# A four-layer graph network on one Trainium2 core: two partial products of layer 0 made between the column sums, and a quarter's tail rows loaded early into two other places

## The chip, the core and the metric

The kernel runs on one core of a Trainium2 chip. A core has a matrix engine (TensorE, PE in the profile), a vector engine (VectorE, DVE), a scalar engine (ScalarE, ACT), a general engine (GpSimd, POOL), and SyncE (SP), which here does nothing but issue transfers. Each has its own instruction queue and works through it in order; DMA engines move data beside them. The metric is the time of one launch in microseconds (us); smaller is better.

## The reference

x is 2708 x 512 and adj is 2708 x 2708, both float32. Four layers follow one another, each adding to x:

```
h = relu(layernorm(x)); x = x + L0(h)    # four times, L0 to L3
L0: deg = adj.sum(1); dinv = (deg+1)^-0.5
    relu( (dinv * (adj + I) * dinv) @ h @ W0 )
L1: (deg^-.5 * adj * deg^-.5) @ h @ W1.T + b1
L2: relu( ((adj+I) scaled by rsqrt of its row sums) @ h @ W2 )
L3: gated sum of attention(adj, h) @ (h W_sa) and adj @ (h W_gcn) + b
```

The large work is (adj + I) @ h, 2708 x 2708 by 2708 x 512, in each layer. In layer 0 the sums of adj's rows are needed before the first product, since h is scaled by them.

## The kernel before

The nodes are cut into four quarters of 677 (five tiles of 128, and a tail of 37 rows that two extra tail tiles collect). The transposed adjacency lies in memory in blocks of 128 x 5 x 339: a quarter of the rows by half a quarter of the columns; the half is called u, 0 or 1. Each layer's product is done by a scheme with seven products of half matrices in place of eight (the outer products 1 to 7: quarters' sums by quarters' sums), and in each of these, for each u, by the same scheme again: `multiply` makes seven inner products. It opens with product 1 in the bank `pa`, then 6 in `pb`, 2 added to `pa`, 7 in `pc`, 5 in `pd`, 4 added to `pc`, 3 added to `pd`. One inner product is five matmuls, recorded as ten, all at L498. `inner_x` (L445) makes the sums s1 to s4 of pieces of h on VectorE, `inner_y` (L461) the sums t1 to t4 of four adjacency blocks. The names XA to XD are views of h; outer product 1 works with XA, whose first half is made of quarter 0's h (five tiles) and whose second half is quarter 1's.

Layer 0 is written out by hand (`first_aggregate`, L637). For quarters 0 and 1 and each u, `degrees` (L315) sums the columns of the adjacency blocks as they are loaded, by matmuls with `first` (L292) into the bank `dg_ps`. `first_h` (L356) turns these sums into columns by one-column matmuls `pd` (L363), makes the scales on VectorE and then h on ScalarE (L223). Blocks for later sums are formed by transfers: `accumulated` (L670) loads a block with a SyncE transfer (L422) and then adds a second block to it with an accumulating GpSimd transfer (L678); VectorE adds the identity where it is wanted (L430), and GpSimd stores the result for later layers (`keep_o`, L418). Places for blocks come from a list `free`.

The tail rows of the adjacency are added to outer products in `tails` (L579): `tail_rows` loads a quarter's rows, both u at once, by two SyncE transfers of 678 columns (L568) into a block from `free`, VectorE adds the identity (L576), TensorE makes four products for each u in four banks `pt` (L554, L559), and VectorE adds these to `agg` (L597). In layer 0 that happens for quarters 0 and 1 between outer products 4 and 5, into the two y22 places; after it, the four blocks for product 5 and u=1 take `t4[3]`, `more[2]` and the same two places (the line with `t1 = [t2u, ...`).

A scheduler builds the instruction order of each engine from the program text and its priorities. `with tc.issue_after(ins)` adds one rule: what stands inside comes after `ins` if both are on the same engine. Transfers in SyncE's and GpSimd's queues are not bound by it when `ins` is on another engine.

Of the kernel before, what the change touches and what calls it, by code (L numbers as in the profile page):

```python
# [37 lines left out]
def gnn_kernel(  # L38
# [317 lines left out]
    def first_h(columns, looped):  # L356

        ts = list(columns)
        n, t0 = len(ts), ts[0]
        span = slice(t0, t0 + n)  # L360
        pd = ps_sm.tile([P, NT], FP, tag="sm", name="pd")
        for s, t in enumerate(ts):
            nc.tensor.matmul(  # L363
                pd[:, s : s + 1], columns[t], ones[:, 0:1], start=True, stop=True
            )
        if looped:
            nc.vector.tensor_copy(deg[:, t0 : t0 + looped], pd[:, :looped])
        if looped < n:
            nc.vector.tensor_scalar(
                deg[:, t0 + looped : t0 + n], pd[:, looped:n], 1.0, None, ALU.add  # L370
            )
        rsqrt(dinv[:, span], deg[:, span], n)
        mv = mv0[:, span, :]
        rstd = rstd_of(mv, n)
        nc.vector.tensor_mul(rstd[:, :n], rstd[:, :n], dinv[:, span])
        sh = shift_of(mv, rstd, n, at_shift)

        fs = slice(0, D // 2), slice(D // 2, D)
        for f in fs if t0 < half else fs[::-1]:
            for s, t in enumerate(ts):  # L380
                normalized(t, h[:, t, :], rstd[:, s : s + 1], sh[:, s : s + 1], f)
# [59 lines left out]


    at_v, at_u2, at_u3, at_end, at_shift, at_y, at_pe = [], [], [], [], [], [], []

    def inner_x(X):  # L445
# [3 lines left out]
        s1, s2, s3, s4 = (  # L449
            spool.tile([P, U * W], FP, tag=f"s{k}", name=f"s{k}")[:, 0 : KT * P].rearrange(  # L450
                "p (k f) -> p k f", k=KT
            )
            for k in (1, 2, 3, 4)
        )
        nc.vector.tensor_sub(s3, x11, x21)
        minus_sum(s2, x22, s3)
        nc.vector.tensor_sub(s1, x21, x22)
        nc.vector.tensor_add(s4, x12, s2)
        return {1: x11, 2: x12, 3: s4, 4: x22, 5: s1, 6: s2, 7: s3}

    def inner_y(blks, u, loops, t3=None):  # L461
        o11, o12, o21, o22 = blks
        if loops:
            add_loops(o11, u, loops)
            add_loops(o22, u, loops)
        t1, t2, t4 = (tpool.tile([P, KT, W], FP, tag="t", name=f"t{k}") for k in (1, 2, 4))
        t3 = o12 if t3 is None else t3
        nc.vector.tensor_add(t1, o12, o11)
        nc.vector.tensor_add(t2, o22, t1)  # L469
        nc.vector.tensor_add(t4, o21, t2)  # L470
        at_y.append(nc.vector.tensor_add(t3, o22, o12).ins)
        return {1: o11, 2: o21, 3: o22, 4: t4, 5: t1, 6: t2, 7: t3}

    def outer_product(p, self_loops, *dests, at=None):
# [12 lines left out]
            multiply(xs_, ys, u, dests)  # L487
            free.extend(blks)

    def multiply(xs_, ys, u, dests, beside=None):  # L490


        cu = slice(u * W, (u + 1) * W)

        def product(ps, q, start):

            for k in range(KT):
                last = nc.tensor.matmul(  # L498
                    ps, xs_[q][:, k, :], ys[q][:, k, :],
                    start=start and k == 0, stop=k == KT - 1, skip_group_check=not start,  # L500
                )
            at_pe.append(last.ins)

        def bank(name):
            return ps_agg.tile([P, W], FP, tag="agg", name=name)

        def give(a, b, ps, part, op):

            if part is not None and (len(dests) > 1 or dests[0][2] != "as it is"):
                s = upool.tile([P, W], FP, tag="s", name="s")  # L510
                nc.vector.tensor_tensor(s, ps, part, op)
                ps, part = s, None
            for fh, ih, how in dests:
                d = agg[:, fh, ih, a, b, cu]
                if part is not None:
                    at_end.append(nc.vector.tensor_tensor(d, ps, part, op).ins)  # L516
                elif how == "added":
                    at_end.append(nc.vector.tensor_add(d, d, ps).ins)
                elif how == "less":
                    at_end.append(nc.vector.tensor_sub(d, ps, d).ins)  # L520
                else:
                    nc.scalar.copy(d, ps)

        pa = bank("pa")
        product(pa, 1, True)
        v = upool.tile([P, W], FP, tag="v", name="v")
        at_v.append(nc.scalar.copy(v, pa).ins)  # L527
        if beside is not None and beside[0] == 1:
            beside[1]()
        pb = bank("pb")  # L530
        product(pb, 6, True)
        u2 = upool.tile([P, W], FP, tag="u2", name="u2", bufs=2)
        at_u2.append(nc.vector.tensor_add(u2, v, pb).ins)
        product(pa, 2, False)
# [6 lines left out]
        product(pd, 5, True)  # L541
        give(1, 1, pd, u3, ALU.subtract)
        if beside is not None and beside[0] == 5:
            beside[1]()
        product(pc, 4, False)
        give(1, 0, pc, u2, ALU.add)
        product(pd, 3, False)
        give(0, 1, pd, u2, ALU.subtract)

    def tail_products(ps, tl, start):  # L550
# [9 lines left out]
                ps[c], h[g, NF + 1, c * P : (c + 1) * P], tl[g, 1, :], start=False, stop=True  # L560
            )

    def tail_rows(self_loops, q):

        blk = free.pop(0)
        both = blk[:, 0 : 2 * U].rearrange("p (s u) w -> p s u w", s=2)
        for s in range(2):
            nc.sync.dma_start(both[:, s], yt[s, :, q])  # L568
        if self_loops:
            o = (KT * P) % W  # L570
            for s, i, c0, n in (
                (0, ident[:, q * R0 : (q + 1) * R0], o, R0),
                (1, again_ident[:, q * R1P + PAD : (q + 1) * R1P], o + R0, R1),
            ):
                d = both[:, s, U - 1, c0 : c0 + n]
                nc.vector.tensor_add(d, d, i)  # L576
        return blk, both

    def tails(self_loops, qs, loaded=None):  # L579


        at = at_pe[-1]
        for n, q in enumerate(qs):
            blk, both = loaded[n] if loaded else tail_rows(self_loops, q)
            for u in range(U):
                tl = both[:, :, u]
                ps = [
                    (ps_agg if c < NC - 1 else ps_out).tile(
                        [P, W], FP, tag="agg" if c < NC - 1 else "out", name="pt"
                    )  # L590
                    for c in range(NC)
                ]
                with tc.issue_after(at) if loaded else nullcontext():
                    tail_products(ps, tl, True)
                for c in range(NC):
                    d = agg[:, c // 2, q // 2, c % 2, q % 2, u * W : (u + 1) * W]
                    at_end.append(nc.vector.tensor_add(d, d, ps[c]).ins)  # L597
            free.append(blk)

    H1 = list(range(0, half))  # L600
    H2 = list(range(half, NT))
# [35 lines left out]
    def first_aggregate(epilogue):  # L637
# [111 lines left out]
        for u in reversed(range(U)):  # L749
# [47 lines left out]
            if u == 1:  # L797
                free += t4
                with tc.issue_after(at_u3[-1]):
                    nc.vector.tensor_sub(XB, XB, XD)  # L800
        for k, y in ((0, y22[0]), (1, y22[1]), (2, y22[0]), (3, y22[1])):
# [422 lines left out]
```

## Time and profile before

| | |
|---|---|
| time, median of three runs | 2138.92 us (2133.96 to 2140.49) |
| the profiled execution | 2133.39 us |
| its span | 2131.5 us |
| mean granted TensorE clock | 0.994 |
| TensorE matmul busy | 2064.2 us, 97%, 7320 instructions |
| VectorE busy | 1413.2 us, 66% |
| ScalarE busy | 406.0 us, 19% |
| GpSimd busy | 182.4 us, 9% |
| DMA moved | 360.86 MB, 169 GB/s on average |

The profile is one execution, taken by the hardware's profiler. A line of the timeline has the start in us from the span's beginning, the duration in us, the engine (SPq is SyncE's queue of transfers), the line of the kernel, the operation, output<-inputs by name, and the number of like instructions put together; the brackets give the idle time before it and what ended it. A line of the list of waits has the engine, what it wanted to do, who released it, and then total us, number and longest.

### The profile page before, as it was taken

The numbers are of one execution on the slowest core, as the hardware profiler recorded it, in microseconds if no ns is written. First come the engines' busy times: TensorE is split into PE (matmuls) and PEld (weight loads), VectorE is DVE, ScalarE is ACT, GpSimd is POOL, SyncE is SP. The second block draws the span as 40 slices with busy tenths as digits, with TensorE's granted clock in tenths as the row PEclk, the third lists the DMA queues.
The fourth block names the chain that finished last, engine by engine and source line by source line (L and its number), as shares of the span: only waits on it lengthen the run. The fifth ranks groups of instructions, "written<-read, shape, count | busy, mean of one in ns | idle before, by whom it ended". The sixth has DMA issues, their size and how long they took to land.

```text
span 2131.5 us, 20035 instructions
## 1 busy us (share of the span) xinstructions
PE 2064.2 (97%) x7320; PEld 1285.7 (60%) x7320; DVE 1413.2 (66%) x2486; ACT 406.0 (19%) x826; POOL 182.4 (9%) x329
## 2 busy tenths in 40 slices
PE   5999989999999999999999999999999999999997
PEld 2566645546666655666664546666777666666664
DVE  3578857667676767766685879967537755666512
ACT  1340000231000010100002120000117533444401
POOL 1111110120000021100002120000001000000001
PEclk9999999999999999999999999999999999999999
DMA  9998594545555443655454565545551233232212
GB/s 369 298 363 250 187 303 167 189 140 209 175 162 169 151 163 140 235 169 160 164 169 141 203 204 196 182 156 167 176 174 59 95 102 116 79 112 90 83 39 65
DMA packets 79154, 360.86 MB, mean 169 GB/s; under 512 B 10588, under 2 KB 14556, under 8 KB 78928
## 3 DMA queue, kind: packets, MB, share of 16 engines
q1 hardware_dynamic: 50096, 245.43, 33.7%
q0 software_dynamic: 28960, 114.15, 16.5%
q8 instruction: 58, 0.95, 0.2%
q14 instruction: 40, 0.33, 0.0%
HBM read 294.61 MB, written 62.15 MB: 167 GB/s over the span
## 4 chain that ended last, share of the span: by engine, by line
issue 45%; PE 39%; DMA 6%; DVE 5%; POOL 3%; ACT 0%; POOLq 0%; SPq 0%; ACTq 0%; DVEq 0%
PE pa L498 9%; PE pc L498 9%; PE pd L498 9%; PE pb L498 5%; PE po L840 4%; DMA obuf<-in_yb_dram 3%; PE pt L554 2%; DMA ends<-xs 1%; PE pg L979 1%; POOL ends L847 1%; POOL xs L866 1%; DVE ends L932 1%; DMA obuf<-in_yt_dram 1%; POOL out_dram L1083 1%; DMA xs<-ends 1%
## 5 line engine op out<-in xcount | busy, mean ns | idle before, releaser
L1131 PE MATMUL pe<-obuf,h 128*128 128x339 f32 x1280 | 372.8, 448 | 0.0
L498 PE MATMUL pa<-obuf,h 128*128 128x339 f32 x1040 | 318.4, 450 | 5.6 <-ACT h L223 4.2
L1131 PEld LDWEIGHTS pe<-obuf,h 128*128 128x128 f32 x1280 | 240.9, 189 | 126.6 <-issue 10.0
L840 PE MATMUL po<-ends,agg 128*128 128x512 f32 x640 | 281.7, 596 | 5.1 <-ACT ends L860 4.8
L498 PEld LDWEIGHTS pa<-obuf,h 128*128 128x128 f32 x1040 | 196.8, 190 | 111.4 <-issue 8.3
L840 PEld LDWEIGHTS po<-ends,agg 128*128 128x128 f32 x640 | 119.6, 190 | 148.3 <-issue 137.5
L498 PE MATMUL pb<-t,s 128*128 128x339 f32 x560 | 172.8, 455 | 3.4 <-DVE t L469 3.4
L1052 ACT ACTIVATE e<-r,nsr 128x339 f32<-128x339 f32 x352 | 170.7, 566 | 27.7 <-DVE obuf L1056 11.6
L498 PE MATMUL pc<-t,h 128*128 128x339 f32 x560 | 169.4, 448 | 2.8 <-DVE u L539 2.8
L498 PE MATMUL pd<-t,s 128*128 128x339 f32 x560 | 169.2, 447 | 0.0
L498 PE MATMUL pd<-obuf,s 128*128 128x339 f32 x550 | 166.5, 448 | 2.6 <-DVE agg L516 2.6
L527 ACT COPY v<-pa 128x339 f32<-128x339 f32 x56 | 24.6, 440 | 751.0 <-PE pa L498 751.0
L498 PEld LDWEIGHTS pb<-t,s 128*128 128x128 f32 x560 | 107.2, 192 | 59.7 <-DVE t L469 4.4
L498 PEld LDWEIGHTS pc<-t,h 128*128 128x128 f32 x560 | 105.8, 189 | 57.8 <-DVE u L539 3.9
L498 PEld LDWEIGHTS pd<-t,s 128*128 128x128 f32 x560 | 105.9, 189 | 54.4 <-issue 0.5
L498 PEld LDWEIGHTS pd<-obuf,s 128*128 128x128 f32 x550 | 104.0, 189 | 56.6 <-DVE agg L516 4.3
L498 PE MATMUL pc<-obuf,s 128*128 128x339 f32 x440 | 133.1, 448 | 0.0
L498 PEld LDWEIGHTS pc<-obuf,s 128*128 128x128 f32 x440 | 83.3, 189 | 42.8 <-issue 0.5
L469 DVE TENSOR_TENSOR t<-obuf,t 128x1695 f32<-128x1695 f32 x55 | 105.4, 1917 | 0.0
L866 POOL DMA_DIRECT2D xs<-ends x66 | 35.9, 544 | 797.4 <-DVE ends L865 714.9
L470 DVE TENSOR_TENSOR t<-obuf,t 128x1695 f32<-128x1695 f32 x52 | 99.6, 1916 | 0.5 <-PE pc L498 0.5
L1148 DVE COPY agg<-pe 128x339 f32<-128x339 f32 x16 | 7.5, 507 | 138.1 <-PE pe L559 138.1
(251 smaller groups left out, 2291.1 us busy)
## 6 DMA issues: line engine op xcount, KB each, us to landing
obuf<-in_yb_dram SPq DMA_DIRECT2D x132, 847.5 KB, 4.5
obuf<-osumt SPq DMA_DIRECT2D x100, 847.5 KB, 4.5
osumt<-obuf POOLq DMA_DIRECT2D x22, 847.5 KB, 10.2
xs<-ends POOLq DMA_DIRECT2D x66, 256.0 KB, 2.3
ends<-xs POOLq DMA_DIRECT2D x66, 256.0 KB, 3.5
obuf<-in_yt_dram SPq DMA_DIRECT2D x32, 339.0 KB, 3.6
obuf<-in_yb_dram POOLq DMA_DIRECT2D x11, 847.5 KB, 10.8
ends<-in_yb_dram SPq DMA_DIRECT2D x9, 847.5 KB, 9.2
```

The lines of the kernel that those rows point to most:

```text
L469: nc.vector.tensor_add(t2, o22, t1)
L470: nc.vector.tensor_add(t4, o21, t2)
L498: last = nc.tensor.matmul(ps, xs_[q][:, k, :], ys[q][:, k, :], start=start and k == 0, stop=k == KT - 1, skip_group_check=not start,)
L527: at_v.append(nc.scalar.copy(v, pa).ins)
L554: nc.tensor.matmul(ps[c], h[:, NF, c * P : (c + 1) * P], tl[:, 0, :], start=start, stop=False)
L840: nc.tensor.matmul(po, cs[c], w_sb[:, c, :], start=(c == 0), stop=(c == NC - 1))
L847: nc.gpsimd.dma_start(xt, src[t])
L866: nc.gpsimd.dma_start(xs[t], xt)
L932: nc.vector.tensor_tensor_reduce(y, h[:, t, :], vs[:, k, :], 1.0, 0.0, ALU.mult, ALU.add, hd[:, t, k : k + 1])
L979: nc.tensor.matmul(pk, cs[c], wg_sb[:, c, k, :], start=(c == 0), stop=(c == NC - 1))
L1052: nc.scalar.activation(e[:, k], row, AF.Exp, bias=nsr[:, t, s : s + 1], scale=1.0)
L1131: nc.tensor.matmul(pe[c], h[:, t, c * P : (c + 1) * P], a, start=(t == 0), stop=False)
```

## The change

Three things in `first_aggregate`, with the functions they use:

1. After quarter 0's h is made, product 1 of outer product 1 is issued for both u, into two `pa` banks, and s3 is formed at once by the new `inner_x3`. `inner_y` for u=0 makes t3 ahead of t1, and product 7 of u=0 is issued behind the one-column matmuls of quarter 1 (`at_pd`). `multiply` takes these banks as `begun`. For u=1 product 7 is issued ahead of product 6, in a bank of `ps_out`. The degree sums take their banks from `ps_out` instead of `ps_agg`.
2. Quarter 0's tail rows for the first tails are loaded long before, by four transfers of 339 columns (L277): those of u=0 into `left`, those of u=1 into the tile `tl` of the pool `ytp`. Quarter 1's rows take the first of the two y22 places.
3. The last two blocks for product 5, u=1, take the two y22 places in the other order.

```diff
@@ first_h
-            nc.tensor.matmul(
+            last = nc.tensor.matmul(
                 pd[:, s : s + 1], columns[t], ones[:, 0:1], start=True, stop=True
             )
+        at_pd.append(last.ins)
...
+    def inner_x3(X):
+        n = half // 2
+        s3 = spool.tile([P, U * W], FP, tag="s3", name="s3")[:, 0 : KT * P]
+        s3 = s3.rearrange("p (k f) -> p k f", k=KT)
+        nc.vector.tensor_sub(s3, X[:, 0:n, 0:P], X[:, 0:n, P : 2 * P])
+        return s3
...
-    def inner_y(blks, u, loops, t3=None):
+    def inner_y(blks, u, loops, t3=None, t3_first=False):
...
+        if t3_first:
+            nc.vector.tensor_add(t3, o22, o12)
         nc.vector.tensor_add(t1, o12, o11)
         nc.vector.tensor_add(t2, o22, t1)
-        nc.vector.tensor_add(t4, o21, t2)
-        at_y.append(nc.vector.tensor_add(t3, o22, o12).ins)
+        at_y.append(nc.vector.tensor_add(t4, o21, t2).ins)
+        if not t3_first:
+            at_y[-1] = nc.vector.tensor_add(t3, o22, o12).ins
...
-    def multiply(xs_, ys, u, dests, beside=None):
+    def multiply(xs_, ys, u, dests, beside=None, begun=None):
...
-        pa = bank("pa")
-        product(pa, 1, True)
+        pa, pc = begun or (None, None)
+        if pa is None:
+            pa = bank("pa")
+            product(pa, xs_[1], ys[1], True)
...
-        pc = bank("pc")
-        product(pc, 7, True)
+        if pc is None:
+            pc = bank("pc")
+            product(pc, xs_[7], ys[7], True)
...
-    def tail_rows(self_loops, q):
-
-        blk = free.pop(0)
-        both = blk[:, 0 : 2 * U].rearrange("p (s u) w -> p s u w", s=2)
-        for s in range(2):
-            nc.sync.dma_start(both[:, s], yt[s, :, q])
+    def tail_rows(self_loops, q, pieces=None):
+        blk = None
+        if pieces is None:
+            blk = free.pop(0)
+            both = blk[:, 0 : 2 * U].rearrange("p (s u) w -> p s u w", s=2)
+            pieces = [both[:, :, u] for u in range(U)]
+            for s in range(2):
+                nc.sync.dma_start(both[:, s], yt[s, :, q])
+        else:
+            for u in range(U):
+                load_tails(q, u, pieces[u])
...
@@ first_aggregate
-            ps = ps_agg.tile([P, W], FP, tag="agg", name="dg_ps")
+            ps = ps_out.tile([P, W], FP, tag="out", name="dg_ps")
...
+            if (q, u) == (0, 1):
+                pas = [bank("pa") for _ in range(U)]
+                for v in range(U):
+                    product(pas[v], XA[:, 0:KT, 0:P], y11[0, 0, v], True)
+                s3 = inner_x3(XA)
             if (q, u) == (1, 0):
-                ys = inner_y([y11[a, b, u] for a, b in QUAD], u, 0, own_t3)
+                ys = inner_y([y11[a, b, u] for a, b in QUAD], u, 0, own_t3, True)
+        pc = bank("pc")
+        with tc.issue_after(at_pd[-1]):
+            product(pc, s3, ys[7], True)
...
-        xs_ = inner_x(XA)
-        multiply(xs_, ys, 0, [p1])
-        ys = inner_y(blks[1], 1, 0, own_t3)
+        xs_ = inner_x(XA, s3)
+        multiply(xs_, ys, 0, [p1], begun=(pas[0], pc))
+        with tc.issue_after(at_u2[-1]):
+            ys = inner_y(blks[1], 1, 0, own_t3)
...
-        multiply(xs_, ys, 1, [p1])
+        pc = ps_out.tile([P, W], FP, tag="out", name="pc")
+        with tc.issue_after(at_pe[-1]):
+            product(pc, xs_[7], ys[7], True)
+        multiply(xs_, ys, 1, [p1], begun=(pas[1], pc))
...
+                y = ytp.tile([P, 2, W], FP, tag="yt", name="tl")
+                with tc.issue_after(at_end[-1]):
+                    early_rows = tail_rows(
+                        True, 0, [left[:, 0 : 2 * W].rearrange("p (s w) -> p s w", s=2), y]
+                    )
...
-            rows = [tail_rows(True, q) for q in (0, 1)]
+            rows = [early_rows, tail_rows(True, 1)]
         tails(True, (0, 1), rows)
-        t1 = [t2u, [t4[3], more[2]] + [free.pop() for _ in range(2)][::-1]]
+        t1 = [t2u, [t4[3], more[2], free.pop(0), free.pop(0)]]
```

More of the change, by code (lines that the diff above doesn't have):

```diff
@@ L443, in gnn_kernel, with inner_x @@
     at_v, at_u2, at_u3, at_end, at_shift, at_y, at_pe = [], [], [], [], [], [], []
-    def inner_x(X):
+    at_pd = []
+    def inner_x3(X):
[4 more added lines that the diff above has]
+        return s3
+    def inner_x(X, s3=None):
         n = half // 2
@@ L448, in inner_x @@
         x21, x22 = X[:, 0:n, P : 2 * P], X[:, n : 2 * n, P : 2 * P]
-        s1, s2, s3, s4 = (
+        s1, s2, s4 = (
             spool.tile([P, U * W], FP, tag=f"s{k}", name=f"s{k}")[:, 0 : KT * P].rearrange(
@@ L452, in inner_x @@
             )
-            for k in (1, 2, 3, 4)
+            for k in (1, 2, 4)
         )
-        nc.vector.tensor_sub(s3, x11, x21)
+        if s3 is None:
+            s3 = inner_x3(X)
         minus_sum(s2, x22, s3)
@@ L488, in outer_product, with bank, product @@
             free.extend(blks)
-    def multiply(xs_, ys, u, dests, beside=None):
-        cu = slice(u * W, (u + 1) * W)
[L495 to L505, printed above, removed]
+    def bank(name):
+        return ps_agg.tile([P, W], FP, tag="agg", name=name)
+    def product(ps, x, y, start):
+        for k in range(KT):
+            last = nc.tensor.matmul(
+                ps, x[:, k, :], y[:, k, :],
+                start=start and k == 0, stop=k == KT - 1, skip_group_check=not start,
+            )
+        at_pe.append(last.ins)
+    def multiply(xs_, ys, u, dests, beside=None, begun=None):
+        cu = slice(u * W, (u + 1) * W)
         def give(a, b, ps, part, op):
@@ L530, in multiply @@
         pb = bank("pb")
-        product(pb, 6, True)
+        product(pb, xs_[6], ys[6], True)
         u2 = upool.tile([P, W], FP, tag="u2", name="u2", bufs=2)
         at_u2.append(nc.vector.tensor_add(u2, v, pb).ins)
-        product(pa, 2, False)
+        product(pa, xs_[2], ys[2], False)
         give(0, 0, pa, None, None)
-        pc = bank("pc")
-        product(pc, 7, True)
+        if pc is None:
+            pc = bank("pc")
+            product(pc, xs_[7], ys[7], True)
         u3 = upool.tile([P, W], FP, tag="u3", name="u3")
@@ L540, in multiply @@
         pd = bank("pd")
-        product(pd, 5, True)
+        product(pd, xs_[5], ys[5], True)
         give(1, 1, pd, u3, ALU.subtract)
@@ L544, in multiply @@
             beside[1]()
-        product(pc, 4, False)
+        product(pc, xs_[4], ys[4], False)
         give(1, 0, pc, u2, ALU.add)
-        product(pd, 3, False)
+        product(pd, xs_[3], ys[3], False)
         give(0, 1, pd, u2, ALU.subtract)
@@ L574, in tail_rows @@
             ):
-                d = both[:, s, U - 1, c0 : c0 + n]
+                d = pieces[U - 1][:, s, c0 : c0 + n]
                 nc.vector.tensor_add(d, d, i)
-        return blk, both
+        return blk, pieces
     def tails(self_loops, qs, loaded=None):
@@ L583, in tails @@
         for n, q in enumerate(qs):
-            blk, both = loaded[n] if loaded else tail_rows(self_loops, q)
+            blk, pieces = loaded[n] if loaded else tail_rows(self_loops, q)
             for u in range(U):
-                tl = both[:, :, u]
+                tl = pieces[u]
                 ps = [
@@ L597, in tails @@
                     at_end.append(nc.vector.tensor_add(d, d, ps[c]).ins)
-            free.append(blk)
+            if blk is not None:
+                free.append(blk)
     H1 = list(range(0, half))
@@ L800, in first_aggregate @@
                     nc.vector.tensor_sub(XB, XB, XD)
+                y = ytp.tile([P, 2, W], FP, tag="yt", name="tl")
+                with tc.issue_after(at_end[-1]):
+                    early_rows = tail_rows(
+                        True, 0, [left[:, 0 : 2 * W].rearrange("p (s w) -> p s w", s=2), y]
+                    )
         for k, y in ((0, y22[0]), (1, y22[1]), (2, y22[0]), (3, y22[1])):
```

## The prediction, made before the changed kernel had run

> **What bounds the kernel now.** I read the page first: the busy shares and the slices.
>
> ```profile
> PE 2064.2 (97%) x7320; PEld 1285.7 (60%) x7320; DVE 1413.2 (66%) x2486; ACT 406.0 (19%) x826; POOL 182.4 (9%) x329
> ...
> PE   5999989999999999999999999999999999999997
> ```
>
> TensorE works 2064.2 of 2131.5 us, so time can be won only by sending it less, by filling its holes, or by raising its clock. The change sends it the same matmuls. The holes are in slice 1 (0 to 53 us) and slice 6 (266 to 320). The list of what TensorE waits for names them:
>
> ```profile
> PE pt L554 <- DVE agg L597: 5.1, 3, 2.7
> ...
> PE pt L554 <- DMA obuf<-in_yt_dram: 4.6, 1, 4.6
> PE pa L498 <- ACT h L223: 4.2, 2, 2.7
> PE pb L498 <- DVE t L469: 3.4, 2, 3.0
> ```
>
> The columns are total, count, longest. Last I read the timeline (start, duration, what; in brackets the idle time before and its releaser) around these waits.
>
> **Part A, products pulled into the start.** The timeline of TensorE:
>
> ```profile
> 34.78 1.98 PE L498 MATMUL pa<-obuf,h 128*128 128x339 f32 x6 [1.41 <-ACT h L223]
> ...
> 56.55 4.75 PE L498 MATMUL pa<-obuf,h 128*128 128x339 f32 x10 [2.75 <-ACT h L223]
> 61.13 1.30 PE L498 MATMUL pb<-t,s 128*128 128x339 f32 x4
> ```
>
> Only u=0's product 1 is made here today. A product is ten records; in a full stream such groups start 2.86 us apart (300.74, 303.59, 306.45), 0.286 us a record. From 61 us on TensorE runs without a hole to 213 us. The change takes two products out of that stream, u=1's product 1 and u=0's product 7: 2 x 2.86 = 5.7 us less to do there. What they cost in the start: product 1 of u=1 stands right behind that of u=0 (34.8 to 40.6), where TensorE then has holes anyway (0.59 at 41.79, 1.34 at 43.73, 0.7 at each of the next three groups, all waits for loads). The degree sum before 41 us ends some 2.5 us later, and so do VectorE's identity adds at 40.08 and t1; VectorE has the slack of the load-paced stretch, and I reckon quarter 1's h 0.3 to 0.7 us later (56.6 for 55.9). Product 7 starts when the degree columns are done, about 54.5, into what was the 2.75 us wait for h. The new t3 and s3 are there by then (t3 only changes places with t1, s3 is 0.83 us by the row at 36.72).
>
> Its price is the clock. Rows by stretch (length, busy time by engine with counts, granted clock, DMA share, GB/s):
>
> ```profile
> 15.50:18.92 3.42, 1.98 (x13) 1.23 (x17) 0.00 (x0) 0.00 (x0) 0.00 (x0) 1.00 1.03 312
> ...
> 53.05:56.46 3.41, 0.75 (x5) 0.66 (x4) 1.62 (x13) 0.87 (x4) 1.06 (x3) 0.50 1.06 413
> 56.46:59.88 3.42, 3.33 (x6) 2.18 (x7) 1.39 (x2) 3.42 (x9) 0.78 (x1) 0.50 1.04 230
> ```
>
> From 53.05 to 59.88 the clock is half, and a record takes 0.57 us: product 7 would take 5.7 us there and the product behind it ends at 59.88 + 3 = 62.9, not at 61.13. The Trainium skill, "TensorE: Matmul & The Clock Gate", section "Part 1: The HAM clock gate", says that the full clock comes only after one busy window of about 3.4 us; this rule speaks against bringing a product forward into a cold stretch. If the 1.96 us of product 7 before 56.46 count as such a window, the full clock is back there, everything ends at 61 and A is worth the whole 5.7. The nearest row is 15.50 to 18.92: 58% busy, and the matmuls after it still start at half rate until 22.3 (durations 0.77 and 0.78, later 0.45). Product 7 fills 57% of its window, so I take the half clock: 5.7 - (62.9 - 61.1) = **4.0 us**, ends 4.0 and 5.7.
>
> It can be eaten up behind 61 us, where DMA is saturated (share 1.01 to 1.04 up to 160 us) and lands when it did. The first landings that a faster TensorE meets are the four accumulated blocks of t3, u=1 (98.6, 103.5, 107.6, 111.7). VectorE adds to the last at 114.4 (2.7 slack), TensorE reads it at 118.8 (7.0). With 4.0 gained VectorE is 1.3 late, inside TensorE's slack of 2.2 to 3.3 at the products behind. Loads of y21 and t2 have over 30 us. A stays.
>
> **Part B, quarter 0's tail rows early.** Timeline of SyncE's queue, of TensorE, and of VectorE, one fence each:
>
> ```profile
> 269.00 5.08 SPq L568 DMA_DIRECT2D obuf<-in_yt_dram  x4
> ```
> ```profile
> 277.21 4.76 PE L554 MATMUL pt<-obuf,h 128*128 128x339 f32 x8 [4.63 <-DMA obuf<-in_yt_dram]
> ...
> 286.81 1.41 PE L554 MATMUL pt<-obuf,h 128*128 128x339 f32 x4 [2.72 <-DVE agg L597]
> ```
> ```profile
> 280.10 0.17 DVE L576 TENSOR_TENSOR obuf<-obuf,again_ident 128x5 f32<-128x5 f32 x1 [2.81 <-DMA obuf<-in_yt_dram]
> 280.18 0.82 DVE L458 TENSOR_TENSOR s<-h,s 128x640 f32<-128x640 f32 x1
> ...
> 283.14 1.92 DVE L468 TENSOR_TENSOR t<-obuf 128x1695 f32<-128x1695 f32 x1
> 286.17 0.17 DVE L576 TENSOR_TENSOR obuf<-obuf,again_ident 128x5 f32<-128x5 f32 x1 [1.11 <-DMA obuf<-in_yt_dram]
> 286.25 1.75 DVE L597 TENSOR_TENSOR agg<-agg,pt 128x339 f32<-128x339 f32 x4
> ```
>
> Four loads of rows, two for each quarter, land at 277.07, 280.07, 283.01 and 286.15. VectorE takes its queue in order: the adds of the last rows (286.17) stand ahead of the adds that empty the tail banks (286.25), so today TensorE waits first for rows (4.63) and then for banks (2.72 here, 1.81 at 292.15). The 9.2 us do not all go: quarter 1's identity adds still stand ahead of the bank adds. Its rows are now the first to be issued, at 269.00, and land as quarter 0's did, 277.07 and 280.07. Behind the second add (280.10) come s4 (0.82), t1 (1.84 start to start) and the first bank add at 282.8, against 286.25: **3.5 us**. TensorE does quarter 0's tails at once from 272.6, then stands some 6.6 us for a bank until 283.3, and the rest follows at its old distance: product 5 starts at 294.3 for 297.77. In that longer hole the clock falls to half again; were it still half in the full stretch behind 288.7, about 1.0 is lost. Ends: 0 if the rows land as late as 286 (below that only the two early identity adds, 0.4 us), and 7 if quarter 0's tails went through with no second wait.
>
> The moved loads cost elsewhere nothing that I find: two rows' worth (0.68 MB, 2 us at 346 GB/s) enter SyncE's queue at 125 to 131, where the y21 loads behind them have 30 us; their identity adds are two of 0.18 us. The layer-3 load leaves that place and stands, with its wait for a tail product, in SyncE's queue at about 288, ahead of a load needed at 294; a bias load now waits in GpSimd's queue until about 293.
>
> **Part C, which block gets which place.** Timeline of SyncE's queue, GpSimd's queue, VectorE and TensorE:
>
> ```profile
> 297.98 0.33 SPq L422 DMA_DIRECT2D obuf<-in_yb_dram  x1
> ```
> ```profile
> 311.05 0.88 POOL L678 DMA_DIRECT2D obuf<-in_yb_dram  x1
> ```
> ```profile
> 320.46 0.61 DVE L430 SCALAR_TENSOR_TENSOR obuf<-ident,obuf 128x45 f32<-128x45 f32 x3 [3.25 <-DMA obuf<-in_yb_dram]
> ...
> 325.92 2.82 DVE L825 TENSOR_TENSOR h<-h 128x2560 f32<-128x2560 f32 x1
> ```
> ```profile
> 325.21 2.35 PE L498 MATMUL pb<-t,s 128*128 128x339 f32 x5 [2.95 <-DVE t L469]
> ```
>
> Two of the four y12 blocks for product 5, u=1, wait for places that the tails hold. The last is loaded at 297.98 (landed 302.90), its accumulation stands in GpSimd's queue behind a store until 311.05 and lands at 320.44; t1, s and t2 follow to 325.16, and pb waits 2.95. After the change one of the two takes the place that is free at 273, and only the other waits for the last tail: load 298, landed 303, accumulation at once (9.4 us by today's) to 312.3 on this clock, where VectorE is ready for it at 316.6. Then VectorE sets the pace: two identity groups to 317.8, t1 to 319.6, s to 320.0, t2 to 321.9; pb starts at 322.0. The next thing late is t3 for pc: behind t2 come 0.93, XC's 2.82, t4 and t3 (1.9 each), to 329.3, where it was 332.4. TensorE stands there about 2 us, so of 2.95 and the half clock at 326.11 to 329.53 (1.7) together **3.1 us** come through. Ends 4.7 and, where the waiting accumulation is as late as today, 0; a loss is case 5 below.
>
> **Sum.** 4.0 + 3.5 + 3.1 = 10.6. All else issues in the same order. The profiled execution took 2133.4 (span 2131.5): 2122.8 after. The median shown is 2138.9, 5.5 above it; with the same distance, **2128.3**. A difference below 0.3% (6.4 us) can't be told from none here.
>
> **Rivals.**
> 1. Forecast, 0.55: 2128.3; own range 2124 to 2133 (0.2% of scatter each way).
> 2. A is given back in the saturated stretch or to the half clock: B + C, 6.6 us, 2132.3 (0.13). For: the DMA share of 1.0 to 160 us. Against: the slacks above.
> 3. B's wait only changes its name: rows of quarter 1 land late (stores and loads crowd 260 to 277 at share 1.01), banks come at 286 again: A + C, 7.1, 2131.8 (0.12).
> 4. More: the clock returns at 56.46 (A 5.7) and the tails run without the second wait (B 7): 15.8, 2123.1 (0.13).
> 5. Slower, 0.07: the one accumulation that still waits for the tails is late. Its load stands in SyncE's queue behind the moved layer-3 load, its accumulation in GpSimd's queue behind a store and the moved bias load. It is reckoned at 312.3 and needed at 317.5; every us later costs one, and from 10.6 us past that, 328.1, the kernel is slower; at 335 it is 7 us slower, 2146.
>
> Cases 2 and 3 lie at the bound of 0.3% and count half to each side: faster 0.55 + 0.13 + 0.12 = 0.80, same 0.13, slower 0.07. The range leaves out case 5 and the edges of the scatter: 2120 to 2136.
>
> **What would show it.** A: ten more pa records before 41 us, a pc at about 54.5 with records of 0.57 us, pb at 62.9 and product 7 of outer product 1 gone after it. B: no wait for rows near 273, one of over 6 us for agg before 283 less A's shift, identity adds of quarter 1 just before 276. C: no wait for t at pb of outer product 5, one of 2 us at its pc. Wrong if new waits for DMA stand between 61 and 213, if the hole at the tails keeps 9 us, or if the last accumulation lands later than its t1 could start.

## The result and the profile after

The changed kernel takes 2126.12 us (median of six runs, 2125.43 to 2128.57); the kernel before, with three more runs beside them, 2135.01 us (six runs, 2133.39 to 2140.49). The ratio is 0.9956, 95% interval 0.9942 to 0.9969: 0.44% faster, 8.9 us between the medians. The forecast was 2128.3 us and 10.6 us less. The profiled execution took 2125.74 us (span 2123.7) against 2133.39 us (span 2131.5): 7.65 us.

The page and the list of what TensorE waits for, of the changed kernel:

```profile
PE 2064.4 (97%) x7320; PEld 1286.0 (61%) x7320; DVE 1412.9 (67%) x2486; ACT 406.0 (19%) x826; POOL 182.3 (9%) x329
```
```profile
PE pt L571 <- DVE agg L621: 7.4, 2, 6.6
...
PE pb L509 <- DVE t L481: 2.6, 2, 2.2
...
PE pc L509 <- DVE ends L484: 1.8, 1, 1.8
```

TensorE is as busy as before to 0.2 us, so all that was won is waiting time. The wait for tail rows (4.6) and the one for h behind quarter 1's degrees (2.75) are gone. One wait for a tail bank, 6.6 us, stands in their place, the wait for t at pb is 2.2 where it was 2.95, and pc of outer product 5 now waits 1.8. TensorE's timeline at the three places:

```profile
34.88 5.98 PE L509 MATMUL pa<-obuf,h 128*128 128x339 f32 x20 [1.39 <-ACT h L223]
...
52.97 0.59 PE L363 MATMUL pd<-ones,across 128*128 128x1 f32 x2 [1.46 <-DVE across L303]
...
54.27 5.66 PE L509 MATMUL pc<-ends,s 128*128 128x339 f32 x10
59.76 3.02 PE L509 MATMUL pa<-obuf,h 128*128 128x339 f32 x10
62.62 3.02 PE L509 MATMUL pb<-t,s 128*128 128x339 f32 x10
```
```profile
278.74 2.63 PE L571 MATMUL pt<-tl,h 128*128 128x339 f32 x4 [6.63 <-DVE agg L621]
...
290.23 3.12 PE L509 MATMUL pa<-obuf,h 128*128 128x339 f32 x10
...
316.95 3.12 PE L509 MATMUL pb<-t,s 128*128 128x339 f32 x10 [2.23 <-DVE t L481]
...
324.20 3.13 PE L509 MATMUL pc<-ends,s 128*128 128x339 f32 x10 [1.84 <-DVE ends L484]
```

Both product 1s (20 records) now stand at 34.88, and product 7 at 54.27 takes 5.66 us for ten records: it runs wholly at half clock. Tails, product 5 and its second half all start earlier, but by different amounts. To see where, I read five marks from every traced execution and take the distances between them, since a difference at one place then does not carry into the next:

- start: from quarter 1's first degree-column matmul (`pd`, 52.97 here) to the first `pb` of outer product 1 (62.62);
- stream: from there to the `pb` of outer product 4, u=0 (249.90);
- tails: from there to the `pb` of product 5's first half (293.20);
- second half: from there to the `pc` of its second half (324.20);
- rest: to the end of the span.

| kernel traced | first mark | start | stream | tails | second half | rest |
|---|---|---|---|---|---|---|
| before | 52.67 | 8.46 | 192.98 | 46.62 | 31.73 | 1799.07 |
| full change | 52.97 | 9.66 | 187.28 | 43.29 | 31.00 | 1799.47 |
| full change, again | 52.63 | 9.83 | 187.27 | 43.52 | 30.56 | 1799.39 |
| A alone | 53.11 | 9.84 | 187.27 | 45.99 | 32.56 | 1798.90 |
| B and C alone | 55.31 | 9.55 | 192.98 | 42.60 | 30.96 | 1803.39 |
| product 1s alone, with B and C | 54.30 | 8.51 | 190.12 | 43.08 | 30.70 | 1798.00 |
| load held back | 52.77 | 8.18 | 186.11 | 42.63 | 28.39 | 1798.21 |
| stores late | 52.96 | 6.60 | 187.13 | 43.14 | 28.50 | 1798.59 |
| loads late | 55.05 | 8.18 | 187.26 | 42.75 | 29.58 | 1803.24 |
| adds late | 52.70 | 9.84 | 187.26 | 38.87 | 36.76 | 1799.10 |
| adds and stores late | 53.05 | 8.18 | 187.26 | 38.25 | 30.38 | 1801.65 |
| all four edits | 52.61 | 6.57 | 187.08 | 39.20 | 27.02 | 1800.51 |
| all four edits, again | 52.88 | 6.51 | 187.03 | 39.58 | 26.94 | 1800.15 |
| before, stores late | 54.56 | 8.52 | 192.96 | 45.79 | 28.42 | 1799.31 |

From the first two rows: stream -5.70, start +1.20, first mark +0.30, tails -3.33, second half -0.73, rest +0.40; together -7.86, the difference of the spans.

### The profile page after: what moved, and what is told of

It is laid out like the page before. It is cut to its first block, busy times and chain, and to the rows that moved or that the text cites. A ratio compares the mean times of both kernels' runs of the same rounds, so it can differ in the third digit from the quotient of the medians.

```text
span 2123.7 us, 20033 instructions
## 1 busy us (share of the span) xinstructions
PE 2064.4 (97%) x7320; PEld 1286.0 (61%) x7320; DVE 1412.9 (67%) x2486; ACT 406.0 (19%) x826; POOL 182.3 (9%) x329
## 4 chain that ended last, share of the span: by engine, by line
issue 45%; PE 39%; DMA 7%; DVE 5%; POOL 3%; ACT 0%; POOLq 0%; SPq 0%; DVEq 0%; ACTq 0%
PE pa L509 9%; PE pc L509 9%; PE pd L509 9%; PE pb L509 5%; PE po L883 3%; DMA obuf<-in_yb_dram 2%; PE pt L571 2%; DMA ends<-xs 2%; PE pg L1022 1%; DMA obuf<-in_yt_dram 1%; POOL ends L890 1%; POOL xs L909 1%; DVE ends L908 1%; PE pt L576 1%; DVE ends L975 1%
```

## The experiments

All are timed against the kernel before on the same chip (2136 to 2137 us there). "Full change" is the changed kernel. The diffs are excerpts; small helpers, such as the lists that collect instructions, are left out.

| kernel | median us | ratio to before | 95% interval |
|---|---|---|---|
| A alone | 2129.47 | 0.9964 | 0.9951 to 0.9977 |
| B and C alone | 2131.28 | 0.9975 | 0.9968 to 0.9982 |
| product 1s alone, with B and C | 2127.77 | 0.9957 | 0.9943 to 0.9971 |
| load held back | 2120.04 | 0.9924 | 0.9909 to 0.9939 |
| stores late | 2122.30 | 0.9934 | 0.9921 to 0.9948 |
| loads late | 2125.99 | 0.9951 | 0.9939 to 0.9964 |
| adds late | 2127.74 | 0.9957 | 0.9944 to 0.9969 |
| all four edits | 2114.96 | 0.9899 | 0.9886 to 0.9913 |
| all four edits, again | 2116.90 | 0.9918 | 0.9905 to 0.9932 |
| before, stores late | 2130.46 | 0.9975 | 0.9968 to 0.9981 |
| adds and stores late | 2120.84 | 0.9940 | 0.9926 to 0.9953 |
| full change, again | 2125.29 | 0.9957 | 0.9944 to 0.9969 |

**The parts by themselves.** A alone: the changed kernel without `early_rows` and its loads, and with the line of `t1` as before:

```diff
-            rows = [early_rows, tail_rows(True, 1)]
+            rows = [tail_rows(True, q) for q in (0, 1)]
```

B and C alone: the two product 1s, t3's place and the banks of the degree sums as before as well as this:

```diff
-        pc = bank("pc")
-        with tc.issue_after(at_pd[-1]):
-            product(pc, s3, ys[7], True)
-        multiply(xs_, ys, 0, [p1], begun=(pas[0], pc))
+        multiply(xs_, ys, 0, [p1])
```

> Part A alone (both product 1s and product 7 early), tails and places as before. Theory, parts are independent up to the tails: pb of the first product starts at 62.6 as in the full change, TensorE runs on without a new hole, gain 4 to 5 us in the profiled execution (ratio 0.9977 to 0.9981). Rival, the gain is taken back at the tails, since quarter 0's rows and what is behind them are paced by transfers: the waits for rows and banks at 270 to 290 grow from 9.2 to 12 or more, gain 0 to 1.5 us.

> Parts B and C without A. Theory, what the full change shows behind its first 62 us: 2.5 us at product 5 and 0.7 at pb of its second half, gain 3 to 3.5 us (ratio 0.9984 to 0.9986), one wait of 6.6 us for a bank at the tails. Rival, B and C are worth the 6.6 us of the prediction when TensorE does not also come 5 us earlier on the transfers: no wait for t at pb, gain 6 to 7 us (ratio 0.997).

A alone: the stream is 187.27 for 192.98 and the start 1.4 longer. At product 5's pb it leads by 4.5 us (296.21 for 300.74), and nothing is given back at the tails (45.99 for 46.62; the waits there are 5.23, 1.98 and 1.81, together 9.0 where they were 9.2). In the second half 0.8 is lost: the half clock lasts longer there (the ten records of pb take 5.93 us where they took 4.81). The span is 3.8 us shorter, a little under the 4 to 5 expected. The theory stands: A's gain is carried through the tails. B and C alone: the tails take 42.60, 4.0 us less than before, and the second half 30.96, 0.8 less; the bank wait is 5.95 us and pb still waits 2.19 for t. (Only the marks of this trace can be used: its execution, 2136.96 us, is the slowest of 21, with half-clock stretches far behind this place.) The rival, that C's full 3.1 would show without A, falls. The medians say 6.9 and 5.1 us, the marks up to that pc 3.7 and 4.8; the two intervals (4.9 to 10.5 and 3.8 to 6.8 of 2136) are too wide to tell a sum from a loss between the parts.

B and C are one change, though. The new line of `t1` takes the only two entries of `free` in the same order as the old one did, and with either line the program is the same, instruction for instruction. The early place comes from part B: quarter 0's rows no longer take one of the two places, so only one of them is held by the tails.

**What product 7's early place is worth.** Product 7 back where it was, both product 1s still early:

```diff
-        pc = bank("pc")
-        with tc.issue_after(at_pd[-1]):
-            product(pc, s3, ys[7], True)
-        multiply(xs_, ys, 0, [p1], begun=(pas[0], pc))
+        multiply(xs_, ys, 0, [p1], begun=(pas[0], None))
```

> The full change with product 7 of outer product 1 back in its old place for both u; only the two product 1s are early. Theory, product 7's advance is worth its 2.86 us less the cold clock that it meets: TensorE starts product 2 at about 57.2, paced by h and half clock, pb near 61.5, product 7 follows later at 2.86, so this is 1.4 to 1.8 us slower than the full change. Rival 1, the half clock takes all of it: the same as the full change within 0.4. Rival 2, the clock costs nothing: 2.8 us slower.

Timeline of TensorE of this kernel, the place where product 7 stood:

```profile
57.85 5.13 PE L509 MATMUL pa<-obuf,h 128*128 128x339 f32 x10 [2.72 <-ACT h L223]
62.81 3.02 PE L509 MATMUL pb<-t,s 128*128 128x339 f32 x10
```

The wait for h is back (2.72). The stream is 190.12, one product (2.85) longer than with product 7 early and one shorter than before; the start is 8.51, 1.15 shorter. So product 7's place is worth 2.85 - 1.15 = 1.7 us, as expected, in these two executions, which both have two half-clock stretches at this place; the two product 1s carry the other 2.8. The medians differ by 1.65, which their scatter can't confirm.

**Why C gave 0.7 for 3.1.** In GpSimd's queue of the changed kernel, the accumulation that waits for the tails is the one at 303.90; VectorE's line shows what it released:

```profile
285.12 0.88 POOL L419 DMA_DIRECT2D osumt<-ends  x1
289.41 0.56 POOL L419 DMA_DIRECT2D osumt<-obuf  x1 [3.41 <-DMA obuf<-in_yb_dram]
...
303.90 0.88 POOL L712 DMA_DIRECT2D obuf<-in_yb_dram  x1 [13.39 <-DMA obuf<-in_yt_dram]
```
```profile
312.20 0.61 DVE L431 SCALAR_TENSOR_TENSOR obuf<-ident,obuf 128x45 f32<-128x45 f32 x3 [2.52 <-DMA obuf<-in_yb_dram]
```

Its load left SyncE at 290.44, as soon as the tails were done, and landed at 303.23 (the bracket of the accumulation names another load): 12.8 us, where before the change the last such load, from 297.98, took 4.9. The two lines of L419 are stores of finished t1 blocks, and they went out ahead of that load. In GpSimd's queue of the kernel before they went out behind it:

```profile
300.65 0.88 POOL L678 DMA_DIRECT2D obuf<-in_yb_dram  x1 [10.00 <-PE pa L498]
301.21 0.88 POOL L418 DMA_DIRECT2D osumt<-ends  x1
310.36 0.56 POOL L418 DMA_DIRECT2D osumt<-obuf  x1 [8.27 <-DMA obuf<-in_yb_dram]
```

The program puts the stores behind the accumulation of the other late block, the one that now has its place early. It left at 300.65 before, at 284.56 after, and the stores moved with it. When the load left, 1.2 MB (counted by whole transfers) had been issued and had not landed in the kernel before, 3.9 MB in the changed one, 1.7 MB of them the stores.

I first asked whether the early place had anything to do with it, by taking it away:

```diff
-                    load_plain(key, a, b, u, blk)
+                    with tc.issue_after(at_load[-1]) if held and (a, b) == (1, 0) else nullcontext():
+                        at_load.append(load_plain(key, a, b, u, blk))
```

> The full change, but the load of the block that has its place free early is held behind the load of the block that waits for the last tail, so both are loaded and accumulated after the tails, as before the change. Theory, the early place did something: without it two loads and two accumulations stand in the saturated stretch behind 290, the last lands 3 to 5 us later than 312.2, and the wait at pb grows from 2.2 to 5 or 7 us; 2 to 5 us slower than the full change. Rival, the transfers are saturated there anyway and the early place only changed their order: last landing within 1 us of 312.2, same time.

Both expectations fell: this kernel, with nothing loaded early, is about 6 us faster than the full change, and its wait at pb is gone (second half 28.39). It was no clean experiment: the scheduler, given the new edge, also moved the stores. Its GpSimd queue:

```profile
292.20 0.87 POOL L713 DMA_DIRECT2D obuf<-in_yb_dram  x1 [13.57 <-DVE agg L855]
294.11 0.87 POOL L713 DMA_DIRECT2D obuf<-in_yb_dram  x1 [1.04 <-DMA obuf<-in_yb_dram]
294.66 0.88 POOL L419 DMA_DIRECT2D osumt<-ends  x1
```

Both accumulations stand ahead of the stores here, and the loads behind the tails landed in 4.6 and 6.3 us. Of the 7.4 us by which its span is shorter, 2.7 are start and stream, where the code is the same and one half-clock stretch fewer fell in each, 2.6 are in the second half, 1.3 in the rest and 0.7 in the tails. So the next two edits moved the crowd and left the places alone. Stores late:

```diff
-        came = accumulated({QUAD[k]: t1[1][k] for k in (0, 1, 3, 2)}, "y12", 1, "y11")
+        accumulated({QUAD[k]: t1[1][k] for k in (0, 1, 3, 2)}, "y12", 1, "y11")
+        came = at_sums[-2]
```

Here `at_sums[-2]` is the accumulation that waits for the tails. Loads late, with the same edge for the layer-3 tail load, and the bias load behind that accumulation:

```diff
-        with tc.issue_after(at_end[-3]):
+        with tc.issue_after(at_end[-3]), tc.issue_after(at_load[-1]):
             rows = [tail_rows(True, q) for q in (2, 3)]
```

> The full change, with one edit: the two stores of finished t1 blocks (0.87 MB each) that stand in GpSimd's queue ahead of the accumulation which waits for the tails come behind it. Theory 1, the last landing (312.2 in the full change) is late because the load behind it took 12.8 us in a stretch crowded with these stores: without them it lands 3 to 5 us earlier, the wait for t at pb (2.2 us) is gone, and 2.0 to 2.5 us of it come through (time about 2123.5). Theory 2, the early place is what crowds it (the run with the load held back was fast because nothing was loaded early): last landing stays within 1.5 us of 312, no gain.

> The full change, with another edit to the same end: the loads of the rows of quarters 2 and 3, the layer-3 load moved by part B and the bias load come behind the load and the accumulation that wait for the tails; the stores stay where they are. Theory 1 (crowd): 1.3 MB fewer ahead of them, at 330 GB/s some 4 us, load 8 to 9 us instead of 12.8, wait at pb 0 to 0.5, gain 1.5 to 2.5 us. Rival: only the stores count, or loads are served by turns in any case, wait at pb within 0.5 of 2.2, no gain.

Stores late, GpSimd's queue, and TensorE's only wait in the second half but one of 0.5 for v:

```profile
296.86 0.85 POOL L712 DMA_DIRECT2D obuf<-in_yb_dram  x1 [13.92 <-PE pc L509]
297.41 0.86 POOL L419 DMA_DIRECT2D osumt<-ends  x1
```
```profile
318.32 3.12 PE L509 MATMUL pc<-ends,s 128*128 128x339 f32 x10 [1.83 <-DVE ends L484]
```

The load takes 9.15 us (287.07 to 296.22), the accumulation lands at 306.31, 16.5 us behind the mark at 289.83, where it was 19.0 in the full change (312.18 less 293.20): 2.5 us earlier, for 3 to 5 expected. The wait for t at pb is gone, and the wait at pc is the one that was forecast. Second half 28.50: 2.5 us less, and 3.2 less than before, the 3.1 of the prediction. Loads late: the load takes 9.9 us, the wait at pb falls to 0.81, second half 29.58, 1.4 less, a little short of what was expected; its median does not differ from the full change's. Theory 1 stands: the load was late because of what had been issued ahead of it, and the stores weigh more than the moved loads.

Then the same order of stores in the kernel before, whose places are the old ones:

```diff
-        came = accumulated({QUAD[k]: t1[1][k] for k in (0, 1, 3, 2)}, "y12", 1, "y11")
+        accumulated({QUAD[k]: t1[1][k] for k in (0, 1, 3, 2)}, "y12", 1, "y11")
+        came = at_sums[-2]
```

> The kernel before, with one edit: the same two stores behind the accumulation that waits for the tails; places of blocks as before. Theory, the order in GpSimd's queue was the limit and the place was not: the accumulation goes out when its load has landed (303 for 311), lands near 312, the wait for t at pb (2.95) and the half clock behind it are gone, pc then waits about 2 for t3: 3 us faster than before. Rival, the place matters: both blocks still come after the tails, last landing 317 or later, no more than 1 us.

Its GpSimd queue:

```profile
306.10 0.86 POOL L679 DMA_DIRECT2D obuf<-in_yb_dram  x1 [2.88 <-DMA obuf<-in_yt_dram]
306.64 0.88 POOL L418 DMA_DIRECT2D osumt<-ends  x1
```

No wait at pb is left, and the second half is 28.42, 3.3 less than before (median 5.6 us less, interval 4.1 to 6.8). The landing was nearer to the rival (318.25, which is 317.2 on the clock of before, not 312), but that is just early enough. So these 3 us do not need the places that parts B and C changed; the order in GpSimd's queue alone brings them.

**What holds the tails.** Quarter 1's identity adds behind the adds that free quarter 0's banks:

```diff
-            rows = [early_rows, tail_rows(True, 1)]
-        tails(True, (0, 1), rows)
+            rows = [early_rows, tail_rows(True, 1, later=True)]
+        tails(True, (0,), rows[:1])
+        with tc.issue_after(at_end[-1]):
+            tail_loops(1, rows[1][1])
+        tails(True, (1,), rows[1:])
```

> The full change, with the identity adds for quarter 1's tail rows put behind the adds that free quarter 0's tail banks on VectorE. Theory of part B in the prediction: these two adds (waiting for rows until 275.5) hold the bank adds, so the 6.6 us wait for a bank falls to about 2.5 and product 5 starts 3.5 to 4.4 us earlier; of this the late landing at pb of its second half takes back most (wait there 2.2 grows to 5 or 6): net 0 to 1 us. Rival 1: it all comes through, 3.5 to 5 us. Rival 2: the adds were not what held the banks, wait still 6 us.

```profile
274.57 2.55 PE L571 MATMUL pt<-tl,h 128*128 128x339 f32 x4 [2.15 <-DVE agg L624]
...
317.99 5.32 PE L509 MATMUL pb<-t,s 128*128 128x339 f32 x10 [7.79 <-DVE t L481]
```

The bank wait falls from 6.63 to 2.15 and the tails take 38.87, 4.4 less. All of it is lost at pb, which waits 7.79: the load now takes 16.0 us (285.91 to 301.93). The longer hole brings the half clock (5.32 for ten records), and the second half is 36.76. What held the banks is settled; of the gain not most but more than all is taken back (1.3 us in the marks; the medians, 1.6 apart, overlap in their runs). With the stores moved too:

> The full change with quarter 1's identity adds late and the stores late, loads and XC as in the full change. With the adds alone the wait at pb grew to 7.8 us, since a load took 16 us. Theory, the stores (1.7 MB) were most of what stood ahead: wait at pb 1 to 3, 5 to 7 us faster than the full change's median in profile terms, time 2119 to 2121. Rival, the moved loads count as much: wait at pb 4 or more, 2122 to 2124.

The wait at pb is 1.61, the tails take 38.25, the second half 30.38; 2120.84 us, 5.3 below the full change: within what the theory expected.

**All of it.** These edits together, and the addition to XC (2.8 us on VectorE) behind t3 of the second half:

```diff
+            if u == 1:
+                with tc.issue_after(at_y[-1]):
+                    nc.vector.tensor_add(XC, XC, XA)
             multiply(xs_, ys, u, p5)
-            if u == 0:
-                with tc.issue_after(at_end[-1]):
-                    nc.vector.tensor_add(XC, XC, XA)
```

> The full change with the stores late, the loads late, quarter 1's identity adds late, and the addition to XC moved behind t3 of product 5's second half, which removes the 1.8 us wait at its pc. If the theories of the single edits hold they add up: 4 at the tails, 2.2 at pb, 1.8 at pc, less what DMA cannot follow: 5 to 8 us faster than the full change, about 2119. If the stretch from 263 to 320 is bound by transfers as a whole, no more than 3 us.

> The full change with all four edits once more, beside it: 2114 to 2117, 10 to 12 us less than the full change, no wait at pb or pc, 2.2 us at the tails.

> The full change once more, unedited, for a comparison on the same chip: 2126 to 2128, wait at the tails 6.6, at pb 2.2, at pc 1.8.

TensorE with all four edits, the waits that are left at the tails and at pb:

```profile
270.81 2.63 PE L571 MATMUL pt<-tl,h 128*128 128x339 f32 x4 [2.15 <-DVE agg L624]
...
307.24 3.12 PE L509 MATMUL pb<-t,s 128*128 128x339 f32 x10 [0.25 <-DVE t L481]
```

No wait at pc is left; tails and second half together take 66.2 and 66.5 us against 78.4 before and 74.3 and 74.1 in the two traces of the full change. 2114.96 and 2116.90 us: 0.8 to 1.0% faster than before, and 8.4 us faster than the full change beside it (2116.90 against 2125.29), a little under the 10 expected there; the first time 5 to 8 had been expected, and it was 11.2. The edits' own part, tails and second half, is 7.6 to 8.1 us. The start, which none of the edits touches, was 3.1 to 3.3 us shorter in both traces, because no half clock fell there, and the rest up to 1.0 longer. This version beats both kernels.

## Why the prediction was right, and where it was not

**A, 4.0 us, right by its steps, and in part by luck.** The two products leave the stream as counted (5.70 of 5.7). The first mark is 0.3 later, of 0.3 to 0.7. Product 7 starts at 54.27 (54.5) and meets the half clock as its nearest row said; pb starts at 62.62 (62.9). Net 4.2. The rule of the Trainium skill that I weighed against A ("TensorE: Matmul & The Clock Gate", "Part 1: The HAM clock gate"), full clock only after a busy window, chose the right end: product 7 ran at half clock. But the traces do not show that one busy stretch is enough. Here the stretch that was 90% busy was half, and the one behind it, busy throughout (56.05 to 59.46), was still half; in the second trace of the full change even a stretch recorded as 100% busy (52.65 to 56.06) was followed by a half one, while with the load held back one such stretch (54.84 to 58.26) brought the full clock. (In the prediction's nearest row the clock reads 1.00 only because that trace has no record of it before 22.3; the durations show the half rate.) Rows by stretch, first of the full change, then of the kernel with the stores late, which is the same code up to here:

```profile
49.22:52.63 3.41, 1.56 (x11) 0.38 (x10) 3.38 (x11) 0.44 (x1) 0.12 (x1) 1.00 1.01 414
52.63:56.05 3.42, 3.08 (x9) 2.46 (x10) 1.54 (x15) 0.30 (x2) 1.67 (x2) 0.50 1.01 414
```
```profile
49.02:52.43 3.41, 1.85 (x12) 0.38 (x10) 3.38 (x11) 0.44 (x1) 0.00 (x0) 1.00 1.03 422
52.43:55.84 3.41, 2.88 (x14) 2.21 (x15) 2.06 (x18) 0.31 (x2) 1.77 (x2) 1.00 1.00 410
```

In the second execution the clock did not fall at all, product 7 took 3.1 us and the start 6.6 us. So the price of product 7's early place is drawn anew in each execution: the start is 6.5 to 6.6 us with no half-clock stretch (of 3.41 us), 8.2 with one, 9.7 to 9.8 with two. The profiled execution drew two, as was reckoned; with none the same code gains 3 us more. The same section says that the windows run freely and that one kernel can show different numbers of cold matmuls from run to run; these traces agree. Rival 2 (A given back) is out: no new wait stands between 61 and 213.

**B, 3.5 us: the mechanism right, 1.0 us too much.** The bank wait stands where it was forecast and is 6.63 us long (6.6); its releaser is the bank adds behind quarter 1's rows:

```profile
275.54 0.17 DVE L600 TENSOR_TENSOR obuf<-obuf,again_ident 128x5 f32<-128x5 f32 x1 [2.80 <-DMA obuf<-in_yt_dram]
...
278.19 1.75 DVE L621 TENSOR_TENSOR agg<-agg,pt 128x339 f32<-128x339 f32 x4
```

Product 5 starts 7.54 us earlier, of which 5.0 come from A and from a 0.79 us wait before the tails that is gone; B's own part is 2.5. The wait for the bank ended 3.1 us earlier by this count, not 3.5. From its end to product 5 it took 11.5 us where it had taken 11.0: what I set aside as an end was the case, the clock is half from 274.50 to 284.74, and the tails behind the wait run slowly (2.63 and 3.51 us for 4 and 8 records; 1.41 and 2.79 before, so 1.9 more), while the second bank wait (1.81), which I had left in, is gone. The run with the adds late shows that the two adds held the banks.

**C, 3.1 us: wrong by 2.4, and this is the step that failed:** "load 298, landed 303, accumulation at once". I took the 4.9 us of that load as its own; they held for the 1.2 MB that stood ahead of it. The load left at the same point of the program as before (290.44, which is 297.98 on the clock of before), but behind 3.9 MB, and took 12.8 us. The share of busy DMA engines, the column before the last, does not tell the two apart: it was full while the load was under way in both. What differs is the stretch ahead of it. Kernel before, then the changed one:

```profile
289.00:298.00 9.00, 7.19 (x33) 3.49 (x34) 7.99 (x12) 0.00 (x0) 0.89 (x1) 1.00 0.75 176
298.00:305.00 7.00, 7.00 (x25) 4.61 (x25) 5.11 (x6) 0.44 (x1) 1.43 (x2) 1.00 1.03 359
```
```profile
284.00:290.00 6.00, 6.00 (x31) 3.22 (x29) 4.82 (x9) 0.00 (x0) 2.02 (x4) 0.94 1.04 259
290.00:297.00 7.00, 7.00 (x31) 4.55 (x25) 5.25 (x6) 0.44 (x1) 0.51 (x1) 1.00 1.02 318
```

The early place itself put the most there: it let the other block's accumulation out early, and with it the two stores that before had left 3.2 and 12.4 us after the load. So the prediction's "All else issues in the same order" failed too. The layer-3 and bias loads that part B moved add 0.6 MB. With A alone, where neither B nor C is in, 1.2 MB stand ahead and the load takes 4.8 us. The last accumulation landed at 312.18, 319.7 on the clock of before, past the point (317.5) from which each us costs one, and pb waited 2.23. This is the mechanism of rival 5, the slower case, at a fifth of the size that it needs to decide. But for the load that rival named only the moved layer-3 load; the stores, which weigh more (2.5 us when they are moved, 1.4 for the loads), it had only ahead of the accumulation, and there little was lost: it left 0.7 us after its load had landed. The further wait, about 2 us for t3 at pc, came as forecast (1.84).

**The sum.** 4.2 + 0.8 + 2.5 + 0.7, less 0.4 in the rest of the program, is 7.9 of the spans, for 10.6. The time came out 2.2 us below the forecast all the same, and that is luck: the median of three from which I took the gain (2138.92) was high by 3.9, since six runs give 2135.01. The fall of 10.6 us that was forecast was one of 8.9 between the medians. The profiled execution, 2125.74, shows the error that the median hides: 2122.8 was forecast for it.

## What to carry to other kernels

A transfer's duration read from a trace holds for the bytes that were ahead of it there; when a change lets one transfer out earlier, look at what stands behind it in its queue and comes out with it, and charge the next load with all of that. Look at this order before changing places: moving two stores behind one accumulation took 3.3 us off the second half of the kernel before, where the change of places took off 0.7. Where a few us are at stake, compare distances between marks within each traced execution, so that a late start or a half-clock stretch of one execution is not read as an effect.

## What the runs showed of the hardware that was not expected

The same code met different clocks. In the ten traces where product 7 is early, the stretch from the degree columns to the first pb took 6.5 to 6.6 us three times, 8.2 three times and 9.7 to 9.8 four times. Within each trace the half-clock stretches begin at whole multiples of 3.413 us from one another. In this grid, the last stretch before the half clock was 46% busy in the full change, 61% with the load held back (51.43 to 54.84) and 63% with adds and stores late (50.98 to 54.39), and stretches of 54% (stores late) and 50% (all four edits, again: 48.95 to 52.36) were not followed by it. So the busy share in the profile does not decide it.

Later in the program, two traces (B and C alone; loads late) have half-clock stretches near 870, 1235 and 1270 us, and take 1803.2 and 1803.4 us for the rest, against 1798.0 to 1799.5 in the traces with none there. Three stretches of 3.41 us at half clock cost 5.1 us by an estimate (half of their length). Both executions were the slowest of all runs of their kernel, so such stretches may be a good part of why runs of one kernel differ by 3 to 9 us; the runs without a trace can't show it. Four other traces have one or two of them (load held back; adds and stores late; both of all four edits) and take 1798.2 to 1801.7.

A load of 0.87 MB took 4.6 to 16.0 us from issue to landing at the same place in the program, by what had been issued before it and had not landed: the last one behind the tails took 4.8 and 4.9 us with 1.2 MB ahead, 6.3 with 1.6 MB, 8.1 to 9.3 with 1.7 MB, 9.1 with 2.2 MB, 9.9 with 2.6 MB, and 12.2 to 16.0 with 3.7 to 3.9 MB.
